# Conditioned 64x64 mixing and a 6-bit dequantised layer: weights loaded in two partition halves, x halves on one queue, and the largest weights sought early

## The chip, the cores and the metric

The kernel runs on one core of a Trainium2 chip. The metric is the device time of one execution in microseconds. Times of the same kernel lie close together: three runs gave 269.41, 269.42 and 270.1 us.

The engines are called as in the profile: PE (TensorE matmuls, with PEld for its weight loads), DVE (VectorE), ACT (ScalarE), POOL (GpSimd) and SP (SyncE, which here only issues DMAs). A "q" behind an engine's name stands for its queue or sequencer. L399 is line 399 of the kernel before.

## The reference

The input x has 64 batches of 64 channels by 1024 features. Each batch has a condition, a number from 0 to 15, that picks one of 16 matrices of 64x64. The result of that product goes through a 1024x1024 layer whose weights are packed as 6-bit numbers, and x is added.

```python
W = weights[condition]                                  # one 64x64 matrix a batch
h = jnp.einsum('bct,bcd->bdt', x, W)                    # 64 x 64 x 1024

p = qweight.reshape(N, groups, 3)                       # four 6-bit values in three words
v0 = p[:, :, 0] & 63
v1 = p[:, :, 0] >> 6 & 63
v2 = p[:, :, 1] & 63
v3 = p[:, :, 2] & 63
w = (unpacked.astype(jnp.float32) - zero_point) * scale # 1024 x 1024

out = x + jnp.einsum('bsk,nk->bsn', h, w) + bias
```

## The kernel before

Two batches make a pair: 64 channels of one batch lie on partitions 0 to 63 (`LO`), those of the other on 64 to 127 (`HI`). There are 32 pairs; two pairs make a group `g`. For each pair PE does two products. Stage 1 multiplies x by the pair's two selected matrices (L399 for pairs 0 and 1, L459 later) into the PSUM tile `ph`. Stage 2 (L483) multiplies the result, split into two f16 parts `hh` and `hl`, by the unpacked 6-bit numbers `q` and accumulates over eight tiles of 128 features in `po`. Scales, zero points and bias are applied afterwards by DVE, ACT and POOL.

The order of the work is written by hand: the tile pool is in manual schedule, so each engine executes in the order in which the function calls stand. The long loop `window(p)` serves pairs 3 to 31; all that comes before it, the start-up for pairs 0 to 2, is spelled out call by call, and the change lies in that part and in the loads.

The words that matter here:

- `w32` holds the 16 matrices in f32. The host's layout gives them twice, once for the 64 channels on partitions `LO` and once on `HI`, so the tile is 128 partitions by 1024 elements, 512 KB (L86).
- `load_pair` loads x of a pair, `load_q` a part of the packed numbers. The order of these calls is the order of SP's queue: `w32`, second half of pair 0, pair 1, the packed numbers, pairs 2 and 3, scale (`scb`), zero point (`zsb`), group 2, bias (`bib`). The first half of pair 0 is issued by ACT's queue behind the conditions `cb`.
- For pairs 0 and 1 stage 1 works in f32 on a block diagonal matrix `wbd`. `early_select(p, j, eng)` reads a batch's condition into a register and copies the matrix into the block (POOL L360, ACT L358).
- `early_weights` (L365, L366), `early_magnitudes` (ACT L377, DVE L379), `early_rows` (L382), `early_bounds` (PE L387) and `early_scales` (L133, L136) find a power of two for the split of `h`; `early_high` (ACT L407) writes `hh`, `early_low` (DVE L414) writes `hl`.
- `early_sums` (ACT L370) sums x over its features for the zero points; `early_feature_sums` (PE L421, DVE L422) multiplies these sums by the block.
- For all later pairs the matrices come from `tab`, an f16 table in two parts, scaled by a power of two for each matrix. It is made by `weights_largest` (DVE L161, the largest magnitude in each matrix row), `weights_turn` and `weights_diagonal` (PE L165, DVE L170 and L172), `weights_bounds` (PE L177), `weights_powers`, `weights_scaled` (DVE L184), `weights_high` (ACT L187) and `weights_low` (DVE L190). After that POOL copies the selections (L232). `weights_hot` and `weights_of_batches` (PE L207) bring these powers to the batches.
- For pairs from 2 on, x is split too: `magnitudes` (ACT L256), `bounds` (PE L260), `scales`, `split_1` (ACT L280, gives `hf`), `split_2` (DVE L290, gives `lf`); `stack_high` and `stack_low` copy the halves into `xa` by SP's DMAs (L302, L303, L307, L308).
- `WARM` dummy matmuls (L542) run on PE before any data is there.

Small PSUM results (`pl`, `pt`, `pw`, `pu`, `pb_`) share two buffers in turn.

Of the kernel before, what the change touches and what calls it, by code (L numbers as in the profile page):

```python
# [8 lines left out]
F32 = mybir.dt.float32  # L9
F16 = mybir.dt.float16  # L10
BF = mybir.dt.bfloat16
# [3 lines left out]
ALU = mybir.AluOpType  # L15
AX = mybir.AxisListType
# [13 lines left out]
def adaln_ffn(ctx: ExitStack, tc: tile.TileContext, x, cond, cw, qw, ws, wz, bias, out):  # L30
# [6 lines left out]
    NG = NP // 2  # L37
    KT = T // P
    LO, HI = slice(0, C), slice(C, P)
    WARM = 42  # L40

    xf = x.rearrange("(i j) c t -> (j c) i t", j=2)
    of = out.rearrange("(i j) c t -> (j c) i t", j=2)
# [14 lines left out]

    xts = {}

    def load_pair(p, ts_=slice(0, T), queue=nc.sync):
        g, i = divmod(p, 2)
        if g not in xts:
            xts[g] = xp.tile([P, 2, T], F32, name="xt")
        queue.dma_start(xts[g][:, i, ts_], xf[:, p, ts_])

    def load_x(g):
        xts[g] = xp.tile([P, 2, T], F32, name="xt")
# [14 lines left out]
    scb = const.tile([P, N], F32, name="scb")  # L83
    bib = const.tile([P, N], F32, name="bib")
    nc.scalar.dma_start(cb, cond.partition_broadcast(NK))
    nc.sync.dma_start(w32, cw)  # L86
    load_pair(0, slice(0, T // 2), nc.scalar)
    load_pair(0, slice(T // 2, T))
    load_pair(1)
    load_q(0)  # L90
    load_q(1)
    load_q(2, 2)
    load_pair(2)
    load_pair(3)
    nc.sync.dma_start(scb, ws.rearrange("n o -> (n o)").partition_broadcast(P))
    nc.sync.dma_start(zsb, wz.rearrange("n o -> (n o)").partition_broadcast(P))
# [45 lines left out]
    def unpack(kt, n=1):  # L142

        w = kt if kt < 2 else kt - 2 if kt < 6 else kt - 4
        to, of_ = q16[:, kt : kt + n, :], qr[:, w : w + n, :]
        if kt in (2, 3, 6, 7):
            nc.vector.tensor_scalar(to, of_, 6 if kt < 4 else 8, 63, ALU.logical_shift_right, ALU.bitwise_and)
        else:
            nc.vector.tensor_scalar(to, of_, 63, None, ALU.bitwise_and)
# [4 lines left out]
    wupb = const.tile([P, NP], F32, name="wupb")  # L154
    wdn = const.tile([P, NK], F32, name="wdn")
    wsc = qp.tile([P, NK, D], F32, name="wsc", bufs=1)
    wmx = const.tile([P, NK], BF, name="wmx")
    tmp = {}

    def weights_largest():  # L160
        nc.vector.tensor_reduce(wmx, w32, AX.X, ALU.max, apply_absolute_value=True)  # L161

    def weights_turn():
        pt = ps_s.tile([NK, P], F32, name="pt", tag="s")
        nc.tensor.matmul(pt, lhsT=wmx, rhs=eye, start=True, stop=True)  # L165
        tmp["pt"] = pt

    def weights_diagonal():
        most = const.tile([NK, 1], F32, name="most")
        nc.vector.tensor_reduce(most, tmp["pt"], AX.X, ALU.max)  # L170
        diag = const.tile([NK, NK], BF, name="diag")
        nc.vector.tensor_scalar(diag, eye[0:NK, 0:NK], most[:, 0:1], None, ALU.mult)  # L172
        tmp["diag"] = diag

    def weights_bounds():
        pw = ps_s.tile([P, NK], F32, name="pw", tag="s")
        nc.tensor.matmul(pw, lhsT=spread, rhs=tmp["diag"], start=True, stop=True)  # L177
        tmp["pw"] = pw

    def weights_powers():  # L180
        powers(tmp["pw"], wup, wdn)

    def weights_scaled():
        nc.vector.tensor_tensor(wsc, w32, wdn.unsqueeze(2).to_broadcast([P, NK, D]), ALU.mult)  # L184
# [31 lines left out]
    def conditions_of(p, eng=nc.sync):  # L216
        conditions[p] = [
            eng.value_load(cb[0:1, 2 * p + j : 2 * p + j + 1], min_val=0, max_val=NK - 1) for j in range(2)
        ]
# [58 lines left out]
    def split_1(g, i, ts_=ALL, sums=None):  # L278

        nc.scalar.activation(  # L280
            st[g]["hf"][:, i, ts_],
            xts[g][:, i, ts_],
            AF.Copy,
            scale=st[g]["down"][:, i : i + 1],
            accum_out=st[g]["xs"][:, i : i + 1] if sums is None else sums,
        )
# [65 lines left out]
    def early_select(p, j, eng):  # L352

        h = (LO, HI)[j]
        k = eng.value_load(cb[0:1, 2 * p + j : 2 * p + j + 1], min_val=0, max_val=NK - 1)  # L355
        to, of_ = wbd[h, p, h], w32[h, ds(k, 1), :].rearrange("p o d -> p (o d)")
        if eng is nc.scalar:
            eng.copy(to, of_)  # L358
        else:
            eng.tensor_copy(to, of_)  # L360

    def early_weights(p):

        wl = const.tile([P, 1], F32, name=f"wl{p}")
        nc.vector.tensor_reduce(wl, wbd[:, p, :], AX.X, ALU.max, apply_absolute_value=True)  # L365
        nc.vector.tensor_scalar(wm[:, p, :], half, wl[:, 0:1], None, ALU.mult)  # L366

    def early_sums(p):
        junk = ap.tile([P, T], BF, name="junk", bufs=1)
        nc.scalar.activation(junk, xts[0][:, p, :], AF.Copy, accum_out=st[0]["xs"][:, p : p + 1])  # L370
# [26 lines left out]
    def early_stage1(p, ph, kts=range(KT)):  # L397
        for kt in kts:
            nc.tensor.matmul(  # L399
                ph[:, kt % ph.shape[1], :, :], lhsT=xts[0][:, p, ts(kt, P)], rhs=wbd[:, p, :], start=True, stop=True  # L400
            )
# [9 lines left out]
    def early_low(p, ph, kts):  # L411
        hh, hl = hs_pair[p]
        for j, h in enumerate((LO, HI)):
            nc.vector.scalar_tensor_tensor(  # L414
                hl[:, kts, h], ph[:, :, j, :], updown[:, p, 1, j : j + 1], hh[:, kts, h], ALU.mult, ALU.subtract
            )
# [23 lines left out]
    def early_out(p):  # L440

        early_minus(p)
        early_res(p)
# [49 lines left out]
    def stage2_tiles(p, kts, ks=range(2)):  # L493
        if p not in pos:
            pos[p] = ps_o[p % 2].tile([P, N], F32, name="po", tag="po")
        products(pos[p], p, kts, ks, BANKS, BANKS)

    def stage2_bank(p, n, ks=range(2), kts=range(KT)):
        if p not in pos:
            pos[p] = ps_o[p % 2].tile([P, N], F32, name="po", tag="po")  # L500
        for k in ks:
            products(pos[p], p, kts, [k], [BANKS[n]], [BANKS[n]])
# [49 lines left out]
    early_select(1, 1, nc.gpsimd)  # L552
    for n in range(2, 8):
        conditions_of(n, nc.gpsimd)
    early_weights(0)
    early_magnitudes(0, 0, HALF[0], nc.scalar)
    early_stage1(0, ph0a, range(0, 4))
    early_magnitudes(0, 1, HALF[1], nc.vector)
    early_rows(0, 0)
    early_rows(0, 1)  # L560
    early_stage1(0, ph0b, range(4, 6))
    early_bounds(0, 2)
    early_stage1(0, ph0b, range(6, KT))
    early_scales(0)
    early_high(0, ph0a, LOWER)
    early_high(0, ph0b, UPPER)
# [6 lines left out]
    stage2_tiles(0, range(0, 2), [0])  # L573
    unpack(2, 2)
    early_low(0, ph0b, UPPER)
    unpack(4, 2)
    stage2_tiles(0, range(0, 2), [1])
    early_rows(1, 0)
    unpack(6, 2)
    weights_largest()  # L580
    early_sums(0)
    stage2_tiles(0, range(2, 3))
    early_bounds(1, 1)
    early_scales(1)
    stage2_tiles(0, range(3, 4))
    magnitudes(1, 0)
    early_high(1, ph1, slice(0, KT))
    stage2_tiles(0, range(4, 5))
    weights_turn()
    weights_diagonal()  # L590
    bounds(1, FIRST)
    scales(1, FIRST)
    stage2_tiles(0, range(5, 6))
    weights_bounds()
    weights_powers()
    early_low(1, ph1, slice(0, KT))
    early.close()
    for n in ("b", "h"):
        ps_o.append(ctx.enter_context(tc.tile_pool(name="ps_" + n, bufs=1, space=bass.MemoryType.PSUM)))
    split_1(1, 0)  # L600
    stack_high(1, FIRST)
    weights_scaled()
    weights_high()
    split_2(1, 0)
    stack_low(1, FIRST)
# [15 lines left out]
    bounds(1, SECOND)  # L621
    scales(1, SECOND)
    early_out(0)
    split_1(1, 1)
    stack_high(1, SECOND)
    split_2(1, 1)
# [8 lines left out]
    stage1_low(2, ph)  # L635
    early_unscales(1)
    weights_hot()
    early_sums(1)


    stage2_bank(2, 0, [0])
# [2 lines left out]
    sums_high(1)  # L644
    sums_low(1, nc.gpsimd)
    split_1(2, 0)
    stage2_bank(2, 0, [1], range(0, 4))
    weights_of_batches()
    early_feature_sums(1)
    stage2_bank(2, 0, [1], range(4, KT))  # L650
    early_zero_points(1)
    unscales(1)
    unscales(2)
# [162 lines left out]
```

## Time and profile before

| | |
|---|---|
| median of three runs | 269.42 us (269.41 to 270.1) |
| profiled execution | 269.44 us |
| its span | 267.6 us |
| granted TensorE clock | 0.999 |
| PE busy | 260.5 us, 97% |
| DVE busy | 201.9 us, 75% |
| ACT busy | 158.6 us, 59% |
| POOL busy | 168.8 us, 63% |
| DMA moved | 54.39 MB, mean 203 GB/s |

The profile is one execution of the program. Its span runs from the first to the last instruction, so the execution's time is 1.84 us above it. Of its views four are used here. The engine row gives busy times. The chain of waits starts at the last instruction and follows at each step what released it; it says which engine sets the end. The timeline lists instructions in order of time: start, duration, engine, line, operation, output and input; in brackets the idle time of the engine just before and what ended it. The table by stretches gives for a window of time the busy time of PE, PEld, DVE, ACT and POOL, the granted clock, the busy share of the 16 DMA engines, and the GB/s that they moved. "To landing" is the time from the issue of a DMA to the moment at which its semaphore shows that all data are there.

### The profile page before, as it was taken

How to read it: one execution, taken by the hardware profiler on the slowest of the kernel's cores; microseconds unless marked ns; L12 is line 12 of the kernel's file. 1: busy time of each engine (PE TensorE's matmuls, PEld its weight loads, DVE VectorE, ACT ScalarE, POOL GpSimd, SP SyncE). 2: the span in 40 equal slices, each digit the busy share in tenths (PEclk: the TensorE clock that was granted, in tenths of full speed). 3: DMA queues.
4: the chain of work that ended last, by engine and by line, in shares of the span. 5: the costliest groups of instructions: out<-in, count | busy, mean ns of one | idle time of the engine just before them, and what ended most of it. 6: DMA issues, size and time to landing. Idle time of an engine off the chain costs nothing.

```text
span 267.6 us, 5724 instructions
## 1 busy us (share of the span) xinstructions
PE 260.5 (97%) x2160; PEld 139.7 (52%) x2160; DVE 201.9 (75%) x271; ACT 158.6 (59%) x283; POOL 168.8 (63%) x96
## 2 busy tenths in 40 slices
PE   6999999999999999999999999999999999999993
PEld 6745545554555555455555455555545555545553
DVE  2889899595986959689595968959597795955543
ACT  3758988666865656675565766556586555624100
POOL 3004353969597895959779595986929296595100
PEclk9999999999999999999999999999999999999999
DMA  6998366957748696488857797677976764551212
GB/s 231 383 360 243 89 127 205 264 169 217 228 127 300 194 308 183 130 278 216 278 168 225 238 272 228 163 248 216 294 209 187 222 154 134 163 159 80 81 53 103
DMA packets 32444, 54.39 MB, mean 203 GB/s; under 512 B 15136, under 2 KB 15392, under 8 KB 32416
## 3 DMA queue, kind: packets, MB, share of 16 engines
q1 hardware_dynamic: 32240, 53.75, 65.7%
q8 instruction: 17, 0.28, 0.4%
q10 hardware_dynamic: 176, 0.27, 0.3%
q14 instruction: 11, 0.09, 0.1%
HBM read 19.93 MB, written 16.78 MB: 137 GB/s over the span
## 4 chain that ended last, share of the span: by engine, by line
PE 92%; DMA 2%; DVE 1%; SPq 1%; ACT 1%; POOLq 1%; issue 1%
PE po L483 77%; PE ph L459 10%; PE pe L483 3%; PE ph L399 1%; DMA cb<-in_itok_B_dram 1%; DMA xa<-lf 1%; POOLq L355 1%; SPq L303 1%; PE pu L330 1%; ACT hf L280 0%; DVE hl L475 0%; ACT hh L471 0%; SPq L307 0%; DVE pe L524 0%; SPq L302 0%
## 5 line engine op out<-in xcount | busy, mean ns | idle before, releaser
L483 PE MATMUL po<-q,hl 128*128 128x512 f16 x496 | 118.6, 379 | 0.0
L483 PE MATMUL po<-q,hh 128*128 128x512 f16 x496 | 118.4, 379 | 0.0
L519 POOL TENSOR_TENSOR xt<-xt,zt 128x1024 f32<-128x1024 f32 x28 | 78.8, 2835 | 51.0 <-ACT zt L517 51.0
L483 PEld LDWEIGHTS <-hl 128*128 128x128 f16 x520 | 50.8, 98 | 59.4
L512 POOL TENSOR_TENSOR xt<-xt,bib 128x1024 f32<-128x1024 f32 x32 | 75.4, 2376 | 5.7 <-DVE lf L290 3.3
L471 ACT CAST hh<-ph 128x1024 f16<-128x1024 f32 (+1 forms) x31 | 30.4, 983 | 79.6 <-PE ph L459 42.5
L483 PEld LDWEIGHTS <-hh 128*128 128x128 f16 x520 | 48.2, 98 | 51.4 <-ACT hh L471 0.3
L524 DVE SCALAR_TENSOR_TENSOR po<-po,u,scb 128x1024 f32<-128x1024 f32 x27 | 34.8, 1287 | 49.2 <-PE po L483 49.2
L290 DVE SCALAR_TENSOR_TENSOR lf<-xt,down,hf 128x1024 f16<-128x1024 f32 x30 | 62.5, 2118 | 0.4 <-ACT hf L280 0.4
L475 DVE TENSOR_TENSOR hl<-ph,hh 128x1024 f16<-128x1024 f32 x30 | 36.5, 1216 | 0.4 <-ACT hh L471 0.4
L459 PEld LDWEIGHTS <-xa 128*128 128x128 f16 x960 | 32.1, 98 | 7.5 <-issue 0.6
L280 ACT ACTIVATE hf<-xt,down 128x1024 f16<-128x1024 f32 x30 | 34.2, 1144 | 1.7 <-DVE down L133 1.7
L529 DVE TENSOR_TENSOR xt<-po,xt 128x1024 f32<-128x1024 f32 x27 | 33.1, 1225 | 1.9
L459 PE MATMUL ph<-wst,xa 128*128 128x64 f16 x960 | 33.0, 193 | 0.5 <-DMA xa<-lf 0.5
L256 ACT ACTIVATE junk<-xt 128x1024 bf16<-128x1024 f32 x30 | 31.7, 1057 | 0.8
L517 ACT ACTIVATE zt<-zsc,hs 128x1024 f32<-128x1024 f32 x28 | 30.5, 1137 | 0.0
L323 ACT ACTIVATE xh<-xh,xs 64x1 f16<-64x1 f16 x52 | 12.4, 287 | 0.5
L232 POOL COPY wst<-tab 128x128 f16 x12 | 2.9, 287 | 15.1 <-DVE tab L190 15.1
L448 POOL TENSOR_TENSOR xt<-xt,res 128x1024 f32<-128x1024 f32 x4 | 9.4, 2356 | 0.0
L483 PE MATMUL pe<-q,hh 128*128 128x256 f16 (+1 forms) x24 | 6.6, 308 | 0.0
L483 PE MATMUL pe<-q,hl 128*128 128x256 f16 (+1 forms) x24 | 6.5, 308 | 0.0
L313 ACT CAST xh<-xs 64x2 f16<-64x2 f32 x30 | 5.8, 192 | 0.4
(86 smaller groups left out, 104.0 us busy)
## 6 DMA issues: line engine op xcount, KB each, us to landing
out_dram<-xt SPq DMA_DIRECT2D x31, 512.0 KB, 3.0
xt<-in_x_dram SPq DMA_DIRECT2D x14, 1024.0 KB, 7.2
xa<-hf SPq DMA_DIRECT2D x26, 256.0 KB, 3.8
xa<-lf SPq DMA_DIRECT2D x26, 256.0 KB, 3.8
xt<-in_x_dram SPq DMA_DIRECT2D x3, 512.0 KB, 7.6
wst<-tab SPq DMA_DIRECT2D x48, 32.0 KB, 3.2
xa<-hf SPq DMA_DIRECT2D x8, 128.0 KB, 3.8
xa<-lf SPq DMA_DIRECT2D x8, 128.0 KB, 2.4
```

Of the source, the lines that this page charges most:

```text
L256: nc.scalar.activation(junk, xts[g][:, i, :], AF.Abs, accum_out=st[g]["l1"][:, i : i + 1])
L280: nc.scalar.activation(st[g]["hf"][:, i, ts_], xts[g][:, i, ts_], AF.Copy, scale=st[g]["down"][:, i : i + 1], accum_out=st[g]["xs"][:, i : ...
L290: nc.vector.scalar_tensor_tensor(st[g]["lf"][:, i, ts_], xts[g][:, i, ts_], st[g]["down"][:, i : i + 1], st[g]["hf"][:, i, ts_], ALU.mult, ...
L459: nc.tensor.matmul(ph[:, kt, j, :], lhsT=st[g]["xa"][:, i, j, ts(kt, P)], rhs=wsts[g][:, i, a, j, :], start=(a == 0), stop=(a == 1),)
L471: nc.scalar.copy(hs_pair[p][0][:, kts, :], ph[:, kts, :])
L475: nc.vector.tensor_tensor(hl[:, kts, :], ph[:, kts, :], hh[:, kts, :], ALU.subtract)
L483: nc.tensor.matmul(po[:, a], lhsT=hs_pair[p][k][:, kt, :], rhs=qT[:, kt, c], start=(kt == 0 and k == 0), stop=(kt == KT - 1 and k == 1),)
L512: nc.gpsimd.tensor_tensor(xt, xt, bib, ALU.add)
L517: nc.scalar.activation(zt, zsc, AF.Copy, scale=st[g]["hs"][:, i : i + 1])
L519: nc.gpsimd.tensor_tensor(xt, xt, zt, ALU.subtract)
L524: nc.vector.scalar_tensor_tensor(po, po, st[g]["u"][:, i : i + 1], scb[:, cols], ALU.mult, ALU.mult)
L529: nc.vector.tensor_tensor(xts[g][:, i, cols], po, xts[g][:, i, cols], ALU.add)
```

## The change

- The weights are loaded in two DMAs: `w32[LO]` first of all, `w32[HI]` behind pair 2.
- Both halves of pair 0 of x are issued by SP, behind `w32[LO]`; ACT's queue issues only the conditions.
- `early_select` copies both diagonal blocks out of `w32[LO]`; the second block is written to the other half of the partitions.
- `weights_largest` reads `w32[LO]` alone and is called ahead of `early_weights(0)`; `weights_turn`, `weights_diagonal`, `weights_bounds`, `weights_powers` and `weights_scaled` are called earlier among the tiles of pair 0.
- There are 36 dummy matmuls instead of 42.
- The bounds of pair 0 stand behind all eight tiles of its stage 1, not after the sixth. Pair 1's bounds and scales stand behind four tiles of stage 2 instead of three.
- `early_sums(1)` is called ahead of `split_1(1, 1)` instead of behind `weights_hot`.
- In the second bank of pair 2, `weights_of_batches` comes behind six tiles instead of four, and `early_feature_sums(1)` behind all eight.

```diff
-    WARM = 42
+    WARM = 36
...
     nc.scalar.dma_start(cb, cond.partition_broadcast(NK))
-    nc.sync.dma_start(w32, cw)
-    load_pair(0, slice(0, T // 2), nc.scalar)
+    nc.sync.dma_start(w32[LO], cw[LO])
+    load_pair(0, slice(0, T // 2))
     load_pair(0, slice(T // 2, T))
     load_pair(1)
     load_q(0)
     load_q(1)
     load_q(2, 2)
     load_pair(2)
+    nc.sync.dma_start(w32[HI], cw[HI])
     load_pair(3)
...
-    wmx = const.tile([P, NK], BF, name="wmx")
+    wmx = const.tile([C, NK], BF, name="wmx")
...
-        nc.vector.tensor_reduce(wmx, w32, AX.X, ALU.max, apply_absolute_value=True)
+        nc.vector.tensor_reduce(wmx, w32[LO], AX.X, ALU.max, apply_absolute_value=True)
...
-        pt = ps_s.tile([NK, P], F32, name="pt", tag="s")
-        nc.tensor.matmul(pt, lhsT=wmx, rhs=eye, start=True, stop=True)
+        pt = ps_s.tile([NK, C], F32, name="pt", tag="s")
+        nc.tensor.matmul(pt, lhsT=wmx, rhs=eye[LO, LO], start=True, stop=True)
...
-        to, of_ = wbd[h, p, h], w32[h, ds(k, 1), :].rearrange("p o d -> p (o d)")
+        to, of_ = wbd[h, p, h], w32[LO, ds(k, 1), :].rearrange("p o d -> p (o d)")
...
+    weights_largest()
     early_weights(0)
     early_magnitudes(0, 0, HALF[0], nc.scalar)
     early_stage1(0, ph0a, range(0, 4))
     early_magnitudes(0, 1, HALF[1], nc.vector)
     early_rows(0, 0)
     early_rows(0, 1)
-    early_stage1(0, ph0b, range(4, 6))
+    early_stage1(0, ph0b, range(4, KT))
     early_bounds(0, 2)
-    early_stage1(0, ph0b, range(6, KT))
     early_scales(0)
...
     unpack(2, 2)
     early_low(0, ph0b, UPPER)
+    weights_turn()
+    weights_diagonal()
     unpack(4, 2)
     stage2_tiles(0, range(0, 2), [1])
     early_rows(1, 0)
     unpack(6, 2)
-    weights_largest()
     early_sums(0)
-    stage2_tiles(0, range(2, 3))
+    stage2_tiles(0, range(2, 4))
+    weights_bounds()
     early_bounds(1, 1)
     early_scales(1)
-    stage2_tiles(0, range(3, 4))
+    weights_powers()
+    weights_scaled()
     magnitudes(1, 0)
     early_high(1, ph1, slice(0, KT))
     stage2_tiles(0, range(4, 5))
-    weights_turn()
-    weights_diagonal()
     bounds(1, FIRST)
     scales(1, FIRST)
     stage2_tiles(0, range(5, 6))
-    weights_bounds()
-    weights_powers()
     early_low(1, ph1, slice(0, KT))
...
     split_1(1, 0)
     stack_high(1, FIRST)
-    weights_scaled()
     weights_high()
...
     early_out(0)
+    early_sums(1)
     split_1(1, 1)
...
     weights_hot()
-    early_sums(1)
...
-    stage2_bank(2, 0, [1], range(0, 4))
+    stage2_bank(2, 0, [1], range(0, 6))
     weights_of_batches()
+    stage2_bank(2, 0, [1], range(6, KT))
     early_feature_sums(1)
-    stage2_bank(2, 0, [1], range(4, KT))
     early_zero_points(1)
```

More of the change, by code (lines that the diff above doesn't have):

```diff
@@ L59, in adaln_ffn, with load_pair @@
     xts = {}
-    def load_pair(p, ts_=slice(0, T), queue=nc.sync):
+    def load_pair(p, ts_=slice(0, T)):
         g, i = divmod(p, 2)
@@ L64, in load_pair @@
             xts[g] = xp.tile([P, 2, T], F32, name="xt")
-        queue.dma_start(xts[g][:, i, ts_], xf[:, p, ts_])
+        nc.sync.dma_start(xts[g][:, i, ts_], xf[:, p, ts_])
     def load_x(g):
```

## The prediction

> **What bounds the kernel now.** I read the page's engine row first, then the chain of waits in order of time, then the timeline of the first 36 us, because the chain changes its nature there. The page says PE is busy 97% of the span, and the chain of waits is PE alone in equal windows of 7.9 us from 35.22 us to the end. No edit lies behind that point, so the change is worth what it moves PE's arrival at 35.22 us.
>
> ```profile
> PE 260.5 (97%) x2160; PEld 139.7 (52%) x2160; DVE 201.9 (75%) x271; ACT 158.6 (59%) x283; POOL 168.8 (63%) x96
> ...
> PE 92%; DMA 2%; DVE 1%; SPq 1%; ACT 1%; POOLq 1%; issue 1%
> ```
>
> Timeline, first microseconds (start, duration, then in brackets the idle time before and its releaser):
>
> ```profile
> 0.75 0.39 SPq L86 DMA_DIRECT2D w<-in_L_cond_weights_dram  x1
> ...
> 1.06 3.89 PEld L542 LDWEIGHTS <-dummy 128*128 128x128 bf16 x42 [1.06 <-DVE one L104]
> ...
> 4.63 0.23 POOL L360 COPY wbd<-w 64x64 f32 x1 [1.87 <-DMA w<-in_L_cond_weights_dram]
> ...
> 6.06 0.69 DVE L379 TENSOR_REDUCE xm<-xt 128x1 f32<-128x512 f32 x1 [0.47 <-DMA xt<-in_x_dram]
> ...
> 6.24 0.63 ACT L377 ACTIVATE junk<-xt 128x512 bf16<-128x512 f32 x1 [1.33 <-DMA xt<-in_x_dram]
> ...
> 6.36 1.58 PE L399 MATMUL ph<-wbd,xt 128*128 128x128 f32 x12 [1.23 <-POOL wbd L360]
> ```
>
> PE's dummy matmuls end at 5.13, then it idles 1.23 us. The view names POOL's copies as releaser, but the two blocks that this matmul reads were in place at 4.91; the third copy belongs to pair 1. What came last is the first half of x: ACT reads it at 6.24, released by its DMA (issued 1.20, 5.0 us to landing). So PE starts when x arrives, and x is late because the queues are full. The stretches (PE, PEld, DVE, ACT, POOL busy, clock, DMA share, GB/s):
>
> ```profile
> 0.00:5.00 5.00, 3.93 (x42) 3.89 (x42) 0.54 (x4) 1.73 (x3) 2.12 (x16) 1.00 0.58 182
> 5.00:10.00 5.00, 3.77 (x36) 3.66 (x34) 3.27 (x12) 2.49 (x7) 0.46 (x2) 1.00 1.02 397
> ```
>
> The DMA engines are saturated from about 4.25 us (397 GB/s at share 1.02); the granted clock is 1.00 throughout. From 6.36 to 28.4 PE has no gap to speak of. Later come two: about 0.5 us around the matmuls of L207 and L421 (28.4 to 29.1), and the stop before stage 1 of pair 4, which the chain follows back to pair 2's first product through hh, hl, scales, hf and four stacking DMAs:
>
> ```profile
> 24.12 0.95 PE ph L459 x32
> 25.09 1.08 ACT hh L471 x2
> ...
> 30.52 1.52 SPq L303
> ...
> 32.72 2.36 DMA xa<-lf
> 35.09 0.14 issue
> 35.22 1.03 PE ph L459 x30
> ```
>
> **The change part by part.** (1) *Less data ahead of x.* The second half of the weights (256 KB) goes behind pair 2. Bytes add up in quarter-microsecond stretches to 0.62 MB by 4.25 us and 2.07 MB by 8.0, 387 GB/s between, so 262 kB fewer are worth 0.68 us to each transfer up to pair 2, and nothing from pair 3 on, where the same bytes are ahead again. Landings before: first x half 6.2, second 6.0, pair 1 7.95, q0 8.65, q1 9.3, q2/3 about 10.45, pair 2 11.9, pair 3 13.2. After: second half 5.4, pair 1 7.27, q0 7.97, q1 8.62, q2/3 9.8, pair 2 11.2, weights' second half 11.9.
>
> The first x half gains more: with the first weights it makes 512 KB at the head of one ring, as the whole weights did before, and they landed at 0.75+3.8 = 4.55 though they shared the engines with ACT's x half. I take 4.55; ends 4.0 (no sharing) and 5.3. The weights' first half lands between 3.5 and 4.55; I take 3.9. Moving the first x half from ACT's queue to SP adds an issue of 0.44 us there, the second weights half another 0.4: pair 1, the q loads and what follows are issued that much later, but they land 6 us and more after issue, so the backlog hides it; without a backlog it would be 0.4 to 0.8 us for each.
>
> **A rule against it.** The row: 512 KB of weights on 128 partitions took 3.8 us to landing where 4 KB of conditions took 2.4, so 1.4 us for the bytes; halving them gives 0.7. [...] No row here loads 64 partitions from HBM. By the row the gain is the 0.68 us above[...]. I go with the row[...].
>
> (2) *Start of PE.* The conditions land at 3.18 and POOL's register loads end at 4.08 (chain), so the copies of pair 0 run at 4.1 to 4.35 instead of 4.63 to 4.91. Copying into the other half of partitions: the nearest row is POOL's xh operation across halves, 0.23 us each like the copies of now; no charge. The 36 dummies end near 4.7: 42 took 4.06 us, and six fewer of the last, quicker ones save some 0.4. PE starts at 4.75 instead of 6.36. Sixteen records of pair 0 at 0.125 us give 6.75, the bounds now behind all eight tiles add 0.03 (their rows come earlier, below). Pair 1 lands at 7.27: PE now waits 0.5 us where before it had 0.4 us in hand. Then 1.87 us (16 at 0.117): stage 2 starts at 9.2, before at 10.30. **Gain 1.1 us**; 1.5 if pair 1 comes 0.5 us sooner.
>
> (3) *Largest weights on VectorE at once.* 1.22 us (row L161; 64 partitions hold the same 1024 elements each; lower end 0.6), at 3.9 to 5.0 in a hole of 1.99 us. Behind it in DVE's queue wait early_weights(0) (0.54), the x half's maximum (0.69), rows (0.36): 5.0, 5.6, 6.3, 6.6. PE's bounds want them at 6.75; cover 0.15. The scales follow at 7.0, hh of four tiles by 8.0, unpack(0) 8.0 to 8.35, unpack(1) 8.65 to 9.05, all before PE's 9.2 (tile 1 is wanted at 9.6). If the weights landed later, 0.15 us of it is free at the bounds and about 1 us at stage 2.
>
> (4) *What follows on DVE.* Back to back from 9.05: hl 0.78, unpack 0.60 (q2/3 at 9.8), hl 0.79, diagonal 0.45, unpack 0.60, rows 0.13, unpack 0.60, to 13.1. PE wants tile 4 at 12.8; it is unpacked at 12.4. Scales, powers and the moved scaling (0.2+0.4+1.13) run to 15.0, so pair 2's scales end at 15.35 instead of 15.7 although the scaling now stands ahead of them; the weights' second half has landed 2 us earlier. hf, hl of pair 1 and split_2 end at 17.9 (before 20.07), weights_low at 19.05 (before 21.28), then POOL's selections. PE's weights_turn, weights_bounds move earlier at 0.1 us each; bounds(1) reuses the PSUM buffer that DVE's powers read until 13.7, PE gets there at 13.7: 0 to 0.2 us. The bounds and scales of pair 1 come after two tiles instead of one; hh of pair 1 is ready at 14.8 and wanted at 16.8. Stage 1 of pair 2 is reached at 23.0 (before 24.12). Its low parts are issued by 18.6, behind loads that ended at 21.45; I expect them at 22. Margin 1.0 us.
>
> (5) *early_sums(1) ahead of split_1(1,1) on ACT* (1.06). Behind it wait split_1, magnitudes(2,0) and the hh casts. It runs at 19.7 to 20.75 while ACT would await DVE's scales of 20.7, which await PE. Cost 0; without that cover 1.06 us at split_1, of which about 0.8 was idle before the hh casts. Leaving the old place frees nothing: hf there waits for DVE's down at 28.7.
>
> (6) *weights_of_batches two tiles later, feature sums at the end of the bank.* The 0.5 us hole goes. But PE then stands 0.5 us earlier at pair 4, whose xa comes by the chain shown, which starts at pair 2's product and moves with it. The wait grows by what the hole gave: net 0. In it L303's issue took 1.52 us where its like take 0.6; nothing in the trace says why. If it is short, up to 0.8 us more; if another issue takes its place, up to 0.4 less.
>
> Sum: 1.1 + 0 + 0 + 0, rounded up to 1.2 for the skew of these ends. Own time of the profiled execution 269.44 (span 267.6 and 1.84 around it), the median 269.42; 269.4 − 1.2 = 268.2.
>
> **The rivals.** [...] *More than the front* (0.24): pair 1 sooner, or the hole at L207 kept as gain because the stacking issues run short: 1.1+0.8 or 1.5+0.5, 267.4. For: one 1.52 us issue sits in that chain. Against: it came again at 43.94. *The change doesn't do it* (0.05): a late second reader, such as stage 1 of pair 2 waiting for xa behind the bias load, gives the front back: 269.3. *Slower* (0.08): the largest-of-weights holds DVE's queue. Stage 2 can't start before the weights' landing plus 4.2 us (1.13 + 0.6 + 0.7 + 0.35 to the rows, 0.45 to the scales, 0.97 to unpack). At 3.9 that is 8.1 and hidden; it decides from 5.0 and loses against before from 6.1, for instance 7.0 gives 11.2: 270.3. For: DVE is in order and the transfer is now the first thing it waits for. Against: twice the bytes landed at 4.55.
>
> **How the numbers follow.** Main case 0.51 (268.2, by itself 267.8 to 268.6). Measurement tells about 0.3% (0.8 us) from no change: faster means below 268.6. Main case nearly whole and the larger gain make 0.80; [...] given back and an edge of the main case make 0.12 for the same; slower 0.08. The range 267.1 to 269.1 leaves out slower, given back and a tail of the larger gain.
>
> **What would show it.** Right: PE's first L399 near 4.75 with no idle time before it, an idle stretch of about 0.5 us on pair 1's DMA near 7, L483 from 9.2, stage 1 of pair 2 near 23.0, the stop before pair 4 longer (about 1.1 us) and the one at L207 gone. Wrong: weights' first half landing at 4.5 or later [...], L399 held by x beyond 5.3, DVE's rows later than PE's bounds, a wait of L459 at 23, or the stop before pair 4 vanishing.

## The result and the profile after

The changed kernel takes 272.95 us (median of five runs, 272.25 to 274.1), the kernel before 269.42 (269.02 to 270.1) beside it: ratio 1.0132, 95% interval 1.0101 to 1.0163. It is slower by some 3.5 us where 1.2 us of gain was forecast. The profiled execution took 272.78 us; its span is 271.0, 3.4 above that of before, and its granted clock 0.994. Line numbers of the changed kernel are mostly one higher (L400 for L399, L460 for L459, L484 for L483).

The engine row and the chain's shares, from the page of the changed kernel:

```profile
PE 263.0 (97%) x2154; PEld 140.6 (52%) x2154; DVE 201.7 (74%) x271; ACT 158.5 (58%) x283; POOL 168.7 (62%) x96
...
PE 90%; DMA 5%; DVE 2%; issue 1%; SPq 0%
```

PE has six matmuls fewer and is busy 2.5 us longer: some matmuls ran slower. DMA's share of the chain went from 2 to 5%. Both are read below.

The front first, from the timeline of the changed kernel (start, duration, in brackets the idle time before and its releaser):

```profile
0.75 0.59 SPq L86 DMA_DIRECT2D w<-in_L_cond_weights_dram  x1
...
1.07 3.76 PEld L543 LDWEIGHTS <-dummy 128*128 128x128 bf16 x36 [1.07 <-DVE one L105]
...
4.69 1.21 DVE L162 TENSOR_REDUCE wmx<-w 64x16 bf16<-64x1024 f32 x1 [1.65 <-DMA w<-in_L_cond_weights_dram]
4.72 0.23 POOL L361 COPY wbd<-w 64x64 f32 x1 [1.95 <-DMA w<-in_L_cond_weights_dram]
...
5.26 2.33 PE L400 MATMUL ph<-wbd,xt 128*128 128x128 f32 x16 [0.17 <-DMA xt<-in_x_dram]
...
9.34 0.59 PE L484 MATMUL po<-q,hh 128*128 128x512 f16 x2
```

PE starts 1.10 us earlier (5.26 against 6.36) with hardly an idle stretch, and stage 2 starts at 9.34 where it started at 10.13 before: 0.8 us gained. (The 16 matmuls at 5.26 took 2.33 us and the next 16 only 2.03; the last section tells why.) Yet half the weights land at 4.65, no sooner than all of them did. The row of before:

```profile
10.13 1.03 PE L483 MATMUL po<-q,hh 128*128 128x512 f16 x4
```

What follows in the changed kernel, on PE, around stage 1 of pair 2:

```profile
22.66 0.59 PE L484 MATMUL po<-q,hl 128*128 128x512 f16 x2
25.20 0.23 PE L460 MATMUL ph<-wst,xa 128*128 128x64 f16 x2 [1.94 <-DMA xa<-lf]
25.64 1.18 PE L460 MATMUL ph<-wst,xa 128*128 128x64 f16 x30 [0.21 <-DMA xa<-lf]
26.63 1.04 PE L484 MATMUL po<-q,hh 128*128 128x512 f16 x2
27.46 1.06 PE L484 MATMUL po<-q,hl 128*128 128x512 f16 x2
28.32 2.62 PE L484 MATMUL po<-q,hh 128*128 128x512 f16 x8
...
33.09 1.16 PE L460 MATMUL ph<-wst,xa 128*128 128x64 f16 x32
```

The kernel before, around stage 1 of pairs 2 and 3:

```profile
23.52 0.59 PE L483 MATMUL po<-q,hl 128*128 128x512 f16 x2
23.96 1.10 PE L459 MATMUL ph<-wst,xa 128*128 128x64 f16 x32
...
30.11 1.09 PE L459 MATMUL ph<-wst,xa 128*128 128x64 f16 x32
```

PE is done with the tile before at 23.25 (before: 24.11) and then waits 1.94 and 0.21 us for the low parts of pair 2's x. Before, it had no wait there. And once it goes on, the stage-2 matmuls take about twice as long: two in 1.04 us against 0.59, for more than 3 us. The stretches of both kernels tell why, and show the DMA engines as well (window, its length, PE busy with its count, granted clock, DMA share, GB/s). Before:

```profile
3.50:4.50 1.00, 1.00 (x13) 1.00 0.89 274
10.50:13.00 2.50, 2.50 (x15) 1.00 0.90 365
19.00:22.00 3.00, 3.00 (x16) 1.00 0.55 127
26.10:29.70 3.60, 3.37 (x19) 1.00 0.54 118
```

After:

```profile
3.50:4.50 1.00, 1.00 (x12) 1.00 1.00 205
10.50:13.00 2.50, 2.50 (x12) 1.00 1.04 244
19.00:22.00 3.00, 3.00 (x16) 1.00 1.06 262
26.10:29.70 3.60, 3.60 (x28) 0.54 0.54 113
```

In the first two rows the half loads pass, the first in 3.5 to 4.5, the second in 10.5 to 13. The engines' share is 1.00 and 1.04, so they are fully busy, and they move 205 and 244 GB/s; before, the second of these stretches moved 365 at a share of 0.90, and 5 to 10 us moved 397 at 1.02. In the third row the queue that before was half empty is full in the changed kernel: the low parts of pair 2's x stand in it. The fourth row is the granted clock: 0.54 for 3.6 us, which costs 3.6 x 0.46 = 1.7 us of PE's time. The chain of waits after:

```profile
18.63 6.87 DMA xa<-lf
...
25.64 1.18 PE ph L460 x30
...
35.10 3.16 DMA xa<-lf
...
38.40 1.03 PE ph L460 x30
```

The low stacks are issued at 18.63, 2 us earlier than before (20.60), and land 6.87 us later, at 25.50, where they took 2.4 us and landed at 23.1 before. The last row stood at 35.22 in the kernel before: the whole loss has come about by then, 3.18 us. In parts: PE is done with the tile ahead of stage 1 of pair 2 earlier by 0.86 (23.25 for 24.11); it then begins stage 1 1.95 us later, where before it began 0.15 us ahead of that end (matmuls overlap), so 2.10 more; from there to stage 1 of pair 3 it needs 7.89 us (25.20 to 33.09) for 6.15 (23.96 to 30.11), so 1.74 more, in which the clock's 1.7 and the second wait of 0.21 lie and from which the hole at L207 is gone; and 0.20 more ahead of pair 4. Together −0.86 + 2.10 + 1.74 + 0.20 = 3.18. The other 0.2 us of the span come behind that.

### The profile page after: what moved, and what is told of

Its sections match the earlier page's. It is cut to its first block, busy times and chain, and to the rows that moved or that the text cites. A ratio compares the mean times of both kernels' runs of the same rounds, so it can differ in the third digit from the quotient of the medians.

```text
span 271.0 us, 5713 instructions
## 1 busy us (share of the span) xinstructions
PE 263.0 (97%) x2154; PEld 140.6 (52%) x2154; DVE 201.7 (74%) x271; ACT 158.5 (58%) x283; POOL 168.7 (62%) x96
## 4 chain that ended last, share of the span: by engine, by line
PE 90%; DMA 5%; DVE 2%; issue 1%; SPq 0%
PE po L484 75%; PE ph L460 10%; DMA xa<-lf 4%; PE pe L484 3%; PE ph L400 2%; DMA xt<-in_x_dram 1%; PE pu L331 1%; DVE hl L415 0%; DVE wsc L185 0%; DVE lf L291 0%; SPq L308 0%; SPq L86 0%; DVE pe L525 0%; DVE xt L530 0%; DVE hs L342 0%
## 5 line engine op out<-in xcount | busy, mean ns | idle before, releaser
L484 PE MATMUL po<-q,hh 128*128 128x512 f16 x496 | 119.6, 382 | 0.0
L484 PE MATMUL po<-q,hl 128*128 128x512 f16 x496 | 119.1, 380 | 0.0
L484 PEld LDWEIGHTS <-hl 128*128 128x128 f16 x520 | 50.7, 98 | 59.6 <-issue 0.5
L484 PEld LDWEIGHTS <-hh 128*128 128x128 f16 x520 | 48.7, 98 | 52.5 <-issue 1.3
L460 PEld LDWEIGHTS <-xa 128*128 128x128 f16 x960 | 32.3, 98 | 10.2 <-DMA xa<-lf 2.4
L460 PE MATMUL ph<-wst,xa 128*128 128x64 f16 x960 | 33.6, 193 | 2.6 <-DMA xa<-lf 2.5
L484 PE MATMUL pe<-q,hh 128*128 128x256 f16 (+1 forms) x24 | 6.6, 308 | 0.0
L484 PE MATMUL pe<-q,hl 128*128 128x256 f16 (+1 forms) x24 | 6.5, 308 | 0.0
```

Of the source, the lines that this page charges most:

```text
L460: nc.tensor.matmul(ph[:, kt, j, :], lhsT=st[g]["xa"][:, i, j, ts(kt, P)], rhs=wsts[g][:, i, a, j, :], start=(a == 0), stop=(a == 1),)
L484: nc.tensor.matmul(po[:, a], lhsT=hs_pair[p][k][:, kt, :], rhs=qT[:, kt, c], start=(kt == 0 and k == 0), stop=(kt == KT - 1 and k == 1),)
```

## The experiments

Diffs are against the changed kernel unless another is named. Ratios are to the kernel before, run beside each. Two theories were set against each other: that loads which reach only 64 partitions pass at half rate and so hold up what stands behind them in SP's queue; and that the new order of calls, the earlier stacking above all, makes the wait by itself.

**The whole weights in one load.**

```diff
-    nc.sync.dma_start(w32[LO], cw[LO])
+    nc.sync.dma_start(w32, cw)
...
-    nc.sync.dma_start(w32[HI], cw[HI])
```

> The changed kernel with one edit undone: the weights come in one DMA on 128 partitions at the head of the queue, nothing behind pair 2; all order changes stay. Theory A (half-partition loads run at half rate: they put some 1.85 us on the queue, so pair 2's xa lands late, PE waits 2.1 us and then loses 1.8 us to a halved clock): the bias load lands near 21.5 again instead of 23.3, stage 1 of pair 2 waits less than 0.3 us, the clock stays 1.00, time 268.5 to 269.5. Rival B (the moved work and the earlier issue of the stacking DMAs are to blame, not the split): the wait and the half clock stay, 272 or more. Rival C (one queue instead of two for x): the same as B, since x stays on SP.

Measured: 269.89 us, ratio 1.0018 [1.0003, 1.0034], a little above the 268.5 to 269.5 expected; 3.1 us of the 3.5 are gone, with every other part of the change kept. The stacks of pair 2 took 2.3 us to landing instead of 7, and PE did not wait there; but PE was late in this profile and the stacks were issued 2 us later than in the changed kernel (20.59 for 18.63), so it does not test the early issue. In the front it had lost what it might have gained:

```profile
3.50:4.50 1.00, 1.00 (x12) 1.00 1.00 305
...
4.25 0.85 PE L542 MATMUL pc<-dummy 128*128 128x128 bf16 x6
5.65 3.75 PE L399 MATMUL ph<-wbd,xt 128*128 128x128 f32 x16 [0.56 <-POOL wbd L360]
```

Sixteen f32 matmuls took 3.75 us where the changed kernel needs 2.33, after a pause of only 0.56 us. They ran at half pace, though the clock's column says 1.00 there (the last section tells why). The first row is the stretch of the weights' load, for the comparison below.

**The split alone.** The kernel before, with its own order of calls and 42 dummies, but with the weights in two loads at the changed places and both blocks copied from `LO`.

> The kernel before with the split alone: first weights half at the head, second behind pair 2, both blocks copied from the first half; x's first half stays on ACT's queue and no work is moved. Theory A: the bias load lands 1 to 2 us later than 21.45, xa of pair 2 lands at 24.5 or later, PE waits 0.5 us or more at stage 1 of pair 2; 270.5 to 273 with the clock drop, 269.5 to 270.5 without. Rival B: 268.7 to 269.4, no wait there.

Measured: 270.5 us, ratio 1.005 [1.0032, 1.0068]. The split costs in the old order too; PE waited 1.19 and 0.25 us ahead of stage 1 of pair 2. It cost less than in the changed kernel: with 1.4 us in all there was no halved clock (1.00 from 24 to 30 us).

**The second half copied instead of loaded.**

```diff
-    nc.sync.dma_start(w32[HI], cw[HI])
...
     for n in range(2, 8):
         conditions_of(n, nc.gpsimd)
+    nc.gpsimd.tensor_copy(w32[HI], w32[LO])
     weights_largest()
```

> The changed kernel without the second weights DMA: POOL copies the first half of the weights to the other 64 partitions after its register loads, in its idle time from about 8.6 us (the two halves hold the same numbers). Theory A: the dip to some 230 GB/s between 10.5 and 13 is gone, the queue is 1.2 us shorter, xa of pair 2 lands near 24.2, PE waits 0.5 to 1.2 us instead of 2.1; 269 to 270.5, lower if the clock doesn't drop. Rival B: no difference, 272 or more. What the copy costs isn't in any trace: [...] nobody waits if it ends by 14.

Measured: 269.83 us, ratio 1.0006 [0.9991, 1.0021]. Taking away the one load of 256 KB and nothing else of the change takes away the loss. PE did not wait at stage 1 of pair 2, where 0.5 to 1.2 us were expected; it came there 1.1 us later than in the changed kernel, after a pause of 0.81 us in the front. The stretch in which the second half had passed:

```profile
10.50:13.00 2.50, 2.50 (x13) 1.00 1.04 404
```

POOL's copy took 1.71 us and nobody waited for it.

**The bias load behind the stacks.**

```diff
-    nc.sync.dma_start(bib, bias.partition_broadcast(P))
...
     stack_low(1, FIRST)
+    nc.sync.dma_start(bib, bias.partition_broadcast(P))
```

> The changed kernel with the bias load (512 KB, first read after 30 us) moved behind the stacking DMAs of pair 2. Theory A: 512 KB less stand ahead of the stacking DMAs, 1.3 us; xa lands near 23.9, PE waits 0.8 us or less, the clock stays 1.00; 269 to 270. Rival D (the stacking DMAs are slow by themselves, however short the queue): they still take 6 us and more to land, 272 or more.

Measured: 271.74 us, ratio 1.0081 [1.0054, 1.0108]. That misses the 269 to 270 expected. The wait at stage 1 of pair 2 fell from 2.15 us to 0.55 and the clock stayed at 1.0, but not because the stacks came early: they still took 5.5 to 5.9 us and landed at 25.2, only 0.3 us before the changed kernel's. PE came 1.1 us later, since the second half of x was late in this profile. Two later waits came on top: the second stacks of group 1 now stood behind the bias and took 4.8 us, and stage 1 of pair 4 began at 37.23. In this profile the loads from pair 2 on came some 1.8 us later than in the changed kernel's (pair 2 at 13.6 for 11.8), which takes up what 512 KB less could give. So this run leaves open how much of the wait is the length of the queue.

**The wait filled with dummy matmuls**, so that PE is busy while the stacks land.

```diff
+    pd = ps_s.tile([P, P], F32, name="pd", tag="s")
+    for _ in range(34):
+        nc.tensor.matmul(pd, lhsT=dummy, rhs=dummy, start=True, stop=True)
     ph = stage1(2)
```

> The changed kernel with 34 dummy matmuls (128x128, about 1.9 us at 56 ns) put on PE just ahead of stage 1 of pair 2, where it waited 2.1 us for xa. They compute nothing that is used. Theory A2 (the wait also costs a halved clock, 26.1 to 29.7 us in the changed kernel's profile): the clock stays 1.00, stage 2 of pair 1's last tiles and pair 2's first run at 0.43 us for two matmuls again; of the 1.8 us some comes back as a longer wait at stage 1 of pair 4: 271.2 to 271.8 against 272.95. Rival: the clock has no part in the loss (one run of the changed kernel had clock 1.000 and 272.25): 272.3 to 273.

Measured: 271.17 us, ratio 1.0061 [1.004, 1.0082], its interval apart from the changed kernel's. The dummies take nothing from the wait, and 1.8 us come back. In the profile the way from stage 1 of pair 2 to that of pair 3 takes 6.12 us instead of 7.89, which is that size and is the share of the halved clock. (The profiled run, 270.27, is faster than the median; in it PE also has no wait ahead of pair 4. And one of the changed kernel's five runs has a mean clock of 1.000 and still took 272.25, so the halved clock is not in all of them; what that one lost instead is not known.) Stage 1 of pairs 2 and 3, and the stretches from 24 us on:

```profile
24.78 1.37 PE L460 MATMUL ph<-wst,xa 128*128 128x64 f16 x32
...
30.90 1.16 PE L460 MATMUL ph<-wst,xa 128*128 128x64 f16 x32
...
24.00:26.00 2.00, 1.88 (x50) 1.00 0.96 289
26.00:28.00 2.00, 2.00 (x16) 1.00 0.67 142
```

**The tail edits alone.** The kernel before, with `early_sums(1)`, `weights_of_batches` and the feature sums at their changed places.

> The kernel before with the two late moves alone: early_sums(1) ahead of split_1(1, 1), weights_of_batches behind six tiles and the feature sums behind the bank. My prediction's working: net 0, since the 0.5 us hole at L207 goes and the wait before pair 4 grows by as much; 269.0 to 269.6. Rival (early_sums(1) holds up split_1 and so the stacking of pair 3 and the casts of pair 2): 269.8 to 270.6.

Measured: 269.41 us, ratio 0.9988 [0.9969, 1.0008]. The hole at L207 was gone and PE waited 0.42 us at stage 1 of pair 4: they give nothing and cost nothing.

**The order of calls alone.** The changed kernel with the whole weights in one load, x's first half on ACT's queue and 42 dummies.

> All moves of the order and both blocks from the first half, but the loads and dummies of before: whole weights in one DMA, x's first half on ACT's queue, 42 dummies. Theory A: no half-rate load, so no loss: 268.8 to 269.6 (the largest weights stand earlier, nothing waits for that). If one queue or 36 dummies made the 0.5 us by which the whole-load variant (269.89) missed before, this is faster than that one by 0.3 to 0.8. Rival B: the order itself costs; 269.9 or more.

Measured: 269.47 us, ratio 0.9997 [0.9977, 1.0017]. The order is not what costs, and it gains nothing either while x comes as late as before (PE started at 6.43). The stacks were issued at 19.54 here, 0.9 us later than in the changed kernel; the early issue itself is tested by the next experiment and the last, where it came at 19.17 and 18.72 without loss.

**The copy, earlier; 42 dummies; the hot weights behind `scales(2)`.** From the third experiment, to keep the front's gain.

> The changed kernel with the second half copied by POOL (1.71 us, now ahead of its register loads), 42 dummies, and weights_hot moved behind the scales of group 2 on VectorE. Theory: no half-rate load behind pair 2, so no wait at stage 1 of pair 2; hf of pair 2 comes 0.6 us sooner because four small operations no longer stand ahead of its scales, so the wait before pair 4 shrinks: 268.4 to 269.2. If that wait is set by the slow stacking issue on SP (1.0 to 2.0 us once in every trace), nothing is gained there: 269.4 to 269.9.

Measured: 269.23 us, ratio 0.9986 [0.9971, 1.0001]. PE started at 5.12 and reached stage 1 of pair 4 at 34.03 without a wait there, 1.2 us earlier than before; 0.3 of it remained at the end. The next windows were longer: stage 1 of pair 5 began 8.45 us later, after a wait for DVE's `hl`, where before it took 7.91. So a delay ahead of 35.22 us is paid in full, as the changed kernel shows, but a gain there is not kept in full, unlike what the prediction's first paragraph takes for granted.

**The same bytes to all partitions.** The kernel with the copied half, and at the place of the second half load one of 256 KB that nobody reads.

```diff
+    wide = const.tile([P, NK // 2, D], F32, name="wide")
+    nc.sync.dma_start(wide, cw[:, 0 : NK // 2, :])
     load_pair(3)
```

> The kernel with the copied half (no second load of the weights) and, at the place in the queue where the changed kernel loads the weights' second half, a load of the same 256 KB that reaches all 128 partitions, into a buffer that nobody reads. Theory (the second half costs because it goes to 64 partitions, at about half the rate): these bytes pass at 400 GB/s or so, in 0.65 us instead of 1.2; the low stacks of pair 2 land about 0.5 us or more before the changed kernel's 25.1 and 25.5 us, the wait ahead of stage 1 of pair 2 falls from 1.9 to 1.3 us or less, the clock is not halved, and the time is 269.8 to 271. Rival (any 256 KB more on the queue at this place cost the same, whatever partitions they go to): the wait stays near 1.9 us, the clock falls, and the time is the changed kernel's 272.9.

Measured: 270.82 us, ratio 1.0029 [1.0008, 1.0051], apart from the changed kernel's 1.0101 to 1.0163. The same number of bytes at the same place costs a fraction if they reach 128 partitions. (The load differs from the half load in one more thing: its rows are 2 KB long instead of 4.) The stretch in which they pass, and PE's wait:

```profile
10.50:13.00 2.50, 2.50 (x13) 1.00 1.06 410
...
24.74 0.23 PE L461 MATMUL ph<-wst,xa 128*128 128x64 f16 x2 [0.99 <-DMA xa<-lf]
25.31 1.03 PE L461 MATMUL ph<-wst,xa 128*128 128x64 f16 x30 [0.34 <-DMA xa<-lf]
```

410 GB/s instead of 244 at nearly the same share (1.06 and 1.04), and the load landed 0.7 us behind pair 2 (11.4 and 12.1) instead of 1.4 (11.8 and 13.2). The stacks landed some 0.3 us before the changed kernel's, less than the 0.5 expected, and PE came half a microsecond later; the wait was 1.33 us for 2.15. That was enough to keep the clock at 1.00 behind it, and so to save 2 us between the two profiles, not 0.8.

**Both halves at the head of the queue.**

```diff
     nc.sync.dma_start(w32[LO], cw[LO])
+    nc.sync.dma_start(w32[HI], cw[HI])
...
-    nc.sync.dma_start(w32[HI], cw[HI])
```

> The changed kernel with the load of the second half moved to the head of the queue, directly behind the first, on the same queue. It shows what two half loads in a row cost where one whole load took until 4.45 us. Theory (half rate for 64 partitions, one after the other): 512 KB pass at some 205 GB/s, in 2.5 us instead of 1.3 to 1.5; the second half and the first half of x land about 1.2 us later than behind a whole load (6.5 to 7 instead of 5.5 us), the PE waits 1 us or more ahead of its first stage-1 records, and the kernel ends at 270.5 to 271.5. Rival (the two halves run beside each other and together have the whole load's rate): x lands at 5.5 as behind the whole load and the time is the whole load's 269.9.

Measured: 270.87 us, ratio 1.0034 [1.0014, 1.0054]. The first half of x landed at 6.64 (2.02 + 4.62), behind a whole load it had landed at 5.5; two half loads in a row cost 1.1 us more than one whole load of the same bytes:

```profile
4.00:4.50 0.50, 0.50 (x8) 1.00 0.93 193
...
6.78 2.02 PE L400 MATMUL ph<-wbd,xt 128*128 128x128 f32 x16 [1.69 <-DMA xt<-in_x_dram]
```

Paid here, the price is the front's gain. The stacks of pair 2 then came without a wait, since PE came later. The profiled run, 269.63, is one of the two fastest of 20; four of the others, of 271.1 to 272.5 us, have a mean clock of 0.990 to 0.994, like the changed kernel's.

**The halves on two queues.**

```diff
     nc.sync.dma_start(w32[LO], cw[LO])
+    nc.scalar.dma_start(w32[HI], cw[HI])
...
-    nc.sync.dma_start(w32[HI], cw[HI])
```

> The changed kernel with the load of the second half issued by ACT on its own queue, beside the first half's on SP's. Theory ([...] two halves on two queues can run beside each other at the whole load's rate): both land by about 5 us, the first half of x by 5.5 to 6, the stacks of pair 2 go through unhindered as with the whole load, and the time is 269.5 to 270. Rival [...]: the halves share 205 GB/s, x lands 1.2 us later, and the time is 270.5 to 271.5 as with both halves on one queue.

Measured: 270.56 us, ratio 1.0025 [1.0000, 1.0051], at the lower end of what the rival gave. The first half of x landed at 6.31, 0.8 us later than behind a whole load; the weights' second half landed at 5.6, where it had landed at 5.5 on the one queue. The engines moved 217 and 221 GB/s in the two halves of 4.0 to 5.0 us, at shares of 1.02 and 0.93, and 240 at 1.06 from 3.5 to 4.5, where the whole load had 305 at 1.00. Here the second queue did not let the halves run beside each other at the whole load's rate. This run's profile holds a second case of the clock. PE waited 1.85 us ahead of its first stage-1 matmul at 6.45:

```profile
6.00:7.00 1.00, 0.55 (x5) 1.00 1.03 387
7.00:8.00 1.00, 1.00 (x9) 0.67 1.01 391
8.00:9.00 1.00, 1.00 (x7) 0.50 1.05 393
9.00:10.00 1.00, 1.00 (x7) 0.50 1.08 406
10.00:11.00 1.00, 1.00 (x8) 0.62 1.02 399
11.00:12.00 1.00, 1.00 (x11) 1.00 1.02 406
```

**A version that is faster than both.** The copied half, POOL's copy placed ahead of `conditions_of`, 42 dummies, everything else as changed.

```diff
-    WARM = 36
+    WARM = 42
...
-    nc.sync.dma_start(w32[HI], cw[HI])
...
+    nc.gpsimd.tensor_copy(w32[HI], w32[LO])
     for n in range(2, 8):
         conditions_of(n, nc.gpsimd)
```

> The changed kernel without the second load (POOL copies the second half from the first, ahead of its reads of the conditions) and with 42 warm-up matmuls instead of 36; it differs from the earlier version of this kind, 269.2, in that the hot weights stay where the change put them. Theory (PE is full from the front on, and what the front gains stays): 268.9 to 269.3, 0.1 to 0.5 below the kernel before. Rival (PE's own work is the floor, and the front's gain is spent again on waits for the second half of x): 269.4, no difference.

Measured: 269.4 us in 22 runs (268.64 to 270.23) against 269.64 in 67 (269.05 to 272.01), ratio 0.9971 [0.9952, 0.999]. It is 0.3% faster. The medians are only 0.24 us apart; the ratio takes in all runs, and 18 of the 67 runs of before took 270.5 us or more, which none of the 22 did. Those runs stand about 1.7 us above the rest. Their mean clock reads 0.999 to 1.000, so a halved clock like the changed kernel's, which lowers the mean to 0.994, is not on record in them. A start at half pace as long as the whole-load run's would cost about that and leave no mark either; no trace of such a run is at hand, so this is a guess. So the 0.3% come mostly from these runs. In the new version's profile PE has no pause in the front:

```profile
1.07 4.66 PE pc L542 x42
5.73 1.87 PE ph L399 x16
```

Not all is well in that profile either. The low stacks of pair 2 landed at 24.5 us (18.72 + 5.79); PE waited 0.74 and 0.24 us for them, without any second load. In the third experiment, with the same loads and an issue 1.1 us later (19.78), they took 2.9 us and were there at 22.6. In the stretch 16 to 19 us the DMA engines of the one had a share of 1.01 at 352 GB/s, those of the other 0.86 at 343. The packets in the traces narrow it down: the four stacks of pair 2 make 256 packets of 2 KB; 240 of them had started by 21.3 us in this version and the last at 23.4, by 21.6 and 22.1 in the third experiment, by 23.0 and 24.6 in the changed kernel. A few last packets make a landing late. Why they come so late, and why equal loads keep the engines busy for different times from one execution to the next, stayed open. So the change's loss is not read from one landing, but from the ratios.

## Why the prediction was wrong

**The step that failed** is the rate of the half loads, in part (1) and under "A rule against it". The prediction took 0.7 us for 256 KB by the row of the whole load, and no row of before loads 64 partitions from HBM. The second half took 1.4 us behind pair 2, and the same bytes to all partitions 0.7. The half load passed at 244 GB/s against 410 in that stretch, and at 205 where a whole load had 305 in the stretch of 3.5 to 4.5 us (other profiles with the same first load read 182 to 277 there; x's first half is issued 0.64 us behind it). That x, right behind in the queue, would make up for a slower half was the author's estimate, and it did not: the shares were 1.00 and 1.04 at 205 and 244 GB/s. Nor did a second queue help: on two queues the second half landed no sooner than on one (5.6 and 5.5 us).

| Step | Forecast | Profile after |
|---|---|---|
| (1) first half of weights lands | 3.9 | 4.65 |
| (1) first half of x lands | 4.55 | 5.1 |
| (1) pair 1 lands | 7.27 | 7.3 |
| (1) pair 2 lands | 11.2 | 11.8 |
| (1) second half of weights lands | 11.9 | 13.2 |
| (1) pair 3 lands | 13.2, as before | 14.24 |
| (2) PE's first stage 1 | 4.75 | 5.26 |
| (2) stage 2 starts | 9.2 | 9.34 |
| (4) PE reaches stage 1 of pair 2 | 23.0 | 23.25 |
| (4) low stacks issued | 18.6 | 18.63 |
| (4) low stacks landed | 22 | 25.5 |

The mistake was worth little where the prediction looked for it and much where it did not. (1) and (2): PE's start came 0.5 us later than forecast, stage 2 only 0.14, since pair 1 landed as forecast and PE, coming later, did not wait for it; against its true start of 10.13 the gain is 0.8 for 1.1. A rival of slower halves, to which the author gave 0.12 and 268.9 us, had the direction right, but priced it at the front alone. (An estimate from rows of before: if half the bytes take as long as the whole, pair 1 lands as before, at 7.95; with 1.87 us of stage 1 behind it stage 2 starts at 9.8, where the prediction had 10.30 for before, so about 0.5 us of gain is left.) What both overlooked is the sentence "nothing from pair 3 on, where the same bytes are ahead again": the bytes were, the time was not. Pair 3 landed 1.0 us later than before (14.24 for 13.2), the bias 1.9 later (23.3 for 21.45), and the low stacks behind it 2.4. At pair 3 this is the half load's rate itself: with the same bytes to all partitions pair 3 landed at 13.4. What came on top further back is not: in the version with the early copy, which has no second load, pair 3 landed 0.7 us sooner than before and the bias still 0.9 later (22.3). Of the wait of 2.15 us, 0.98 is there without a second load and 1.33 with the same bytes at 410 GB/s, one profile each; the half load's rate adds the last 0.8, and only with these did the clock fall.

(4) expected the low stacks at 22, with a margin of 1.0 us. It put their landing close behind loads that it took as ended at 21.45, as before. But stacks that are issued at 18.6, 2 us sooner, meet a queue that is still full, where those of before met one half empty (share 0.55 from 19 to 22 us), and they are themselves transfers of 64 partitions: 200 to 221 GB/s passed from 19 to 22 us in the third experiment, the version with the early copy and the same-bytes kernel, at shares of 1.00 to 1.04. (They also go from SBUF to SBUF; no run tells which of the two sets their rate.) An earlier issue gave no earlier landing. The forecast had named this wait ("a wait of L459 at 23") and given it 0.05 as a rival with the price of the front's gain alone.

The price was the second thing missed. Beyond the wait of 2.15 us PE lost 1.7 us to the halved clock, for which the prediction had no term; its row of before showed a pause of 1.23 us with the clock at 1.00. The slower rival was another mechanism, the largest-of-weights in DVE's queue, and did not occur: DVE ran L162 at 4.69 and PE never waited for its rows.

**What held.** (3) the reduction hidden, 1.21 us; (5) and (6) at net 0, as the tail edits alone show; the order of calls as such, also 0; POOL's and ACT's copies across halves at 0.23 and 0.24 us each. That the whole load in the changed order is not faster than before either says that the change had little to win: without the half load's delay it comes out at no difference.

## What to carry to other kernels

Ask of each transfer not only how many bytes it has but how many partitions it reaches: here a half load, to 64 of 128 partitions, took 1.4 us for 256 KB, twice what the same bytes took over 128 partitions, and so delayed what stood behind it in the queue, up to a wait 10 us later, far from the place that the split was made for. If the other half holds a copy, let an idle engine make it. And if PE comes earlier to a place where it waits for a transfer, price the wait with what follows it: here a wait of 2.15 us halved PE's clock (0.54 over 3.6 us) and cost 1.7 us more, while one of 1.33 left it at 1.00.

## What the runs showed of the hardware that was not expected

- *The clock fell behind some pauses of PE of about 2 us.* A pause of 1.94 us, with 0.21 more behind two matmuls, was followed by half clock from 26.4 to 29.8 us in the changed kernel, and one of 1.85 us by half clock from 7.3 to 10.8 with the halves on two queues. Pauses of 1.23 (before), 1.33 (same bytes to all partitions) and 1.69 (both halves at the head) left it at 1.00 in their profiles. The entries of the clock in the traces of before and after go some way to show how this goes together. Between two changes lie 3.41, 20.48 and 242.35 us in the one of after and 262.83 in the one of before, which is 1, 6, 71 and 77 steps of 3.41 us. The step at whose end the clock fell held 2.15 us of idle time in the changed kernel; with the two queues it held 1.85, if the step ahead of 7.3 us was as long there. Idle time of 1.44 us in all (the split alone) did not bring the clock down. In the pause of 1.69 the clock rose: the six dummies ahead of it took 0.85 us (0.50 with the two queues, at the higher pace), the 16 f32 matmuls behind it 2.02. If it rose at the end of a step too, no step held all of that pause. So in these runs the idle time within one step seems to go with the fall, an inference from two falls, and where the steps begin differs between executions (4.34 us before, 5.89 after).
- *PE starts at half pace, and the column does not show it.* The entries of the clock begin only some microseconds into each of these two traces, at 4.34 us before and at 5.89 in the changed kernel, and where there is no entry the column reads 1.00. Ahead of the first entry the dummies start 107 ns apart and stage 1's f32 matmuls 214 (changed kernel), behind it 56 (before) and 112. In the whole-load run 16 f32 matmuls from 5.65 took 3.75 us instead of 2.0, and the next 16, from 9.29, 2.15 instead of 2.02; by these times half pace lasted to about 9.55 (an estimate: 0.13 us more is 0.26 us at half pace). With the halves on two queues it was over by 4.1 (six dummies in 0.50 us), with both halves at the head by 6.78. Why it lasted longer in the whole-load run, after a pause of 0.56 us, was not tested.
- *A stacking DMA with a long issue on SP*: 1.52 us before (L303, at 30.52) where its like take 0.6, 1.41 in the changed kernel (L309, at 35.10). In most other profiles there was one too, of up to 2.04 us (the bias load behind the stacks, L307 at 32.66); with the wait filled there was none from 25 to 38 us. No cause was found.
- *A copy of 64 x 1024 f32 to the other half of the partitions* took POOL 1.71 us in the third experiment and 1.03 or 1.04 in the later kernels, in the same-bytes kernel at the same place. In the third experiment DVE unpacked weights for 0.67 us (L147, from 13.41) while the copy ran (from 13.28). The difference is 0.67 us too; whether the one comes from the other was not tested.
